# An output ring cut into three equal slots instead of four stores a tile

## The chip, the cores and the metric

The kernel runs on one core of one Trainium2 chip. The metric is the time of the core in microseconds (us), the median over several executions. One further execution is taken by the hardware profiler, which gives a page and a trace. Engines are named as the page names them: PE for matrix multiply, PEld for its weight loads, DVE for elementwise work, ACT, POOL, and SP, which here only issues transfers.

## What is computed

```python
# inputs (4096, 32, 64) f32, W (496, 64, 64) f32
i_idx, j_idx = np.triu_indices(32, k=1)          # the 496 pairs i < j
vi = inputs[:, i_idx, :]
vj = inputs[:, j_idx, :]
vdotw = jnp.einsum('bpd,pde->bpe', vi, W)
inter = vdotw * vj
return inter.reshape(B, -1)                      # (4096, 31744) f32
```

For each of 4096 batch rows and each pair (i, j) of 32 fields, field i (64 numbers) goes through the pair's 64x64 matrix and is multiplied elementwise with field j. The output holds 520 MB; the inputs hold 42 MB. So this kernel writes far more than it reads.

## The kernel before

The batch is cut into NT = 32 tiles of 128 rows, one row to a partition. A tile's output is 31744 columns wide: 496 units of D = 64 columns, one unit for each pair. Units are the measure of everything below.

For a field i, all its pairs (i, j) lie side by side, 31 - i units of them, and need the same left operand. Fields are taken two at a time: pair of fields p holds fields 2p and 2p+1, which lie in the upper and the lower 64 partitions of one transposed block of x. The matmul (L221) multiplies the transposed field with up to 512 columns of weights into one PSUM bank, for both fields into two neighbouring banks. The eight PSUM banks are handed out two at a time (`take_banks`), so PE can be four steps ahead of DVE.

DVE then multiplies both banks with the matching columns of x in one instruction and writes the product into the SBUF tile `ring`. The instruction of L231 writes two runs of columns at once, one for field 2p and one for field 2p+1, whose places in the output lie a whole row of pairs apart. L239 writes single runs, for the pieces that have no partner.

The order of work in a tile is p = 0 to 15, and in each p the column chunks from left to right. At p = 3 the second half of the tile's x is transposed on PE (L181) and copied out by ACT (L182), at p = 9 the first half of the next tile's x.

The `ring` holds 28160 columns (440 units) in each partition. The list STORES groups the field pairs into four stores a tile, of 118, 102, 123 and 153 units. Each store's place in the ring is taken when its first product is made: directly behind the store before, or at column 0 where it would not fit behind. A DVE instruction that writes to a place in the ring waits until the stores that last read that place have landed in HBM. After a group's last product the store is issued on SP (L245):

```python
        for s, group in enumerate(STORES):
            if at + store_w[s] > RING:
                at = 0
            osb = ring[:, at : at + store_w[s]]
            at += store_w[s]
```

A store is one transfer of 128 rows, one to a partition, each contiguous in SBUF and in HBM. Eight rows go to each of the 16 DMA engines.

Inputs come in beside this. The weights (8 MB) are loaded once, in five pieces, on SP at the start. Tiles of x go into three slots, some of them loaded from ACT's queue (L156) and 13 of them from POOL's queue (L117). The POOL loads spread their rows unevenly over the DMA engines, with small "nudge" transfers that set at which engine the next one begins. A load of x waits until DVE has done with the tile that was in its slot.

Of the kernel before, what the change touches and what calls it, by code (L numbers as in the profile page):

```python
# [9 lines left out]
F32 = mybir.dt.float32  # L10
ALU = mybir.AluOpType

P = 128
BANK = 512
BANKS = 8

STORES = [[0, 1], [2, 3], [4, 5, 6], [7, 8, 9, 10, 11, 12, 13, 14, 15]]

LOADS = [[0], [1], [2, 3], [4, 5, 6], [7, 8, 9, 10, 11, 12, 13, 14, 15]]


FIRST_HALF_AT, SECOND_HALF_AT = 9, 3
RING = 28160

DMA_ENGINES = 16
LIGHT = 4
# [7 lines left out]
def x_slots(NT):  # L34


    loads = [[(0, 0)]]
    for t in range(1, NT, 2):
        if t + 1 == NT:
            loads.append([(t, 1)])  # L40
        elif loads[-1][-1] == (t - 1, 2):
            loads.append([(t + 1, 0), (t, 1)])
        else:
            loads.append([(t, 1), (t + 1, 2)])
    return loads


@with_exitstack
def pair_bilinear_kernel(
    ctx: ExitStack,  # L50
    tc: tile.TileContext,
    x: bass.AP,
    w: bass.AP,
    out: bass.AP,
    F: int,
    D: int,
):

    nc = tc.nc
    NT = out.shape[1] * 2 // (F * (F - 1) * D)
    NPR = F // 2

    width = [(F - 1 - i) * D for i in range(F)]
    off = [sum(width[:i]) for i in range(F)]
    cols = sum(width)


    woff = [i % 2 * D + sum(width[i % 2 : i : 2]) for i in range(F)]
    store_w = [sum(width[2 * p] + width[2 * p + 1] for p in g) for g in STORES]

    const = ctx.enter_context(tc.tile_pool(name="const", bufs=1))
    psum = ctx.enter_context(tc.tile_pool(name="ps", bufs=1, space=bass.MemoryType.PSUM))

    ident = const.tile([P, P], F32, tag="ident", name="ident")
    make_identity(nc, ident)

    def runs(tl, a, b, n):  # L100

        ap = tl[:, a : a + n]
        return bass.AP(ap.tensor, ap.offset, [list(ap.ap[0]), [b - a, 2], list(ap.ap[1])])

    xbuf = const.tile([P, 3 * F * D], F32, tag="x", name="x")
    x_loads = x_slots(NT)
    pads = (DMA_ENGINES + 1) * PAD
    tile_sizes = [P * F * D + (pads if t in LIGHT_TILES else 0) for t in range(NT)]
    x_sizes = [sum(tile_sizes[t] for t, s in load) for load in x_loads]
    slot = {t: xbuf[:, ts(s, F * D)] for load in x_loads for t, s in load}  # L110

    nudges = [const.tile([DMA_ENGINES, 16], F32, tag=f"nudge{i}", name=f"nudge{i}") for i in range(2)]
    cursor = 0

    def from_pool(out, in_):

        tc.keep_in_program_order(nc.gpsimd.dma_start(out=out, in_=in_))  # L117

    def from_engine(e):

        nonlocal cursor
        k = (e - cursor) % DMA_ENGINES
        if k:
            nudge = nudges[e == LIGHT + 1]
            from_pool(
                nudge[:k].rearrange("p (h c) -> p h c", h=2)[:, :, :4],
                x[: k * 8].rearrange("(p h c) -> p h c", p=k, h=2),
            )
        cursor = e

    def load_beside(at, xt, lap):

        nonlocal cursor
        most = DMA_ENGINES - 1
        for e, k, rows, p in (
            (PAIRS_FROM[lap % len(PAIRS_FROM)], 2, REST, most * HEAD),
            (LIGHT + 1, most, HEAD, 0),
        ):
            from_engine(e)
            n = rows * F * D  # L140
            blocks = x[at : at + k * (n + PAD)].rearrange("(k c) -> k c", k=k)
            from_pool(xt[p : p + k * rows], blocks[:, :n])
            at += k * (n + PAD)
            cursor = (e + k) % DMA_ENGINES

    def load_x(load):

        at = sum(x_sizes[: x_loads.index(load)])
        parts = [[(t, s)] for t, s in load] if any(t in LIGHT_TILES for t, s in load) else [load]
        for part in parts:  # L150
            t, s = part[0]
            n = len(part) * F * D
            if t in LIGHT_TILES:
                load_beside(at, slot[t], LIGHT_TILES.index(t))
            else:
                nc.scalar.dma_start(  # L156
                    out=xbuf[:, s * F * D : s * F * D + n],
                    in_=x[at : at + P * n].rearrange("(p c) -> p c", p=P),
                )
            at += sum(tile_sizes[t] for t, s in part)  # L160

    pring = psum.tile([P, BANKS * BANK], F32, tag="pring", name="pring")
    bank = 0

    def take_banks(n):

        nonlocal bank
        if bank + n > BANKS:
            bank = 0
        got = pring[:, bank * BANK : (bank + n) * BANK]  # L170
        bank = (bank + n) % BANKS
        return got

    xT = const.tile([P, NPR * P], F32, tag="xT", name="xT")

    def transpose_x(xt, g):

        n = 2 * BANK // P
        pt = take_banks(2)
        for c in range(n):  # L180
            nc.tensor.transpose(pt[:, ts(c, P)], xt[:, ts(n * g + c, P)], ident)  # L181
        nc.scalar.copy(xT[:, ts(g, 2 * BANK)], pt)  # L182

    ring = const.tile([P, RING], F32, tag="ring", name="ring")
    at = 0

    load_x(x_loads[0])
    w_sb = const.tile([P, sum(width[0::2])], F32, tag="w", name="w")
    done = 0
    for g in LOADS:  # L190

        upto = woff[2 * g[-1]] + width[2 * g[-1]]
        nc.sync.dma_start(out=w_sb[:, done:upto], in_=w[:, done:upto])
        done = upto

    transpose_x(slot[0], 0)
    for t in range(NT):
        xt = slot[t]
        for load in x_loads:
            if min(load)[0] == t + 1:  # L200
                load_x(load)
        for s, group in enumerate(STORES):
            if at + store_w[s] > RING:
                at = 0
            osb = ring[:, at : at + store_w[s]]
            at += store_w[s]
            o0 = off[2 * group[0]]
            for p in group:
                if p == SECOND_HALF_AT:
                    transpose_x(xt, 1)  # L210
                if p == FIRST_HALF_AT and t + 1 < NT:
                    transpose_x(slot[t + 1], 0)
                first = (width[2 * p] - 1) % BANK + 1
                for c1 in range(first, width[2 * p] + 1, BANK):
                    n = first if c1 == first else BANK
                    c0 = c1 - n
                    odd = width[2 * p + 1] and c1 > D
                    pm = take_banks(2)
                    for h in range(1 + bool(odd)):
                        a = woff[2 * p + h] + c0 - h * D  # L220
                        nc.tensor.matmul(  # L221
                            pm[:, h * BANK : h * BANK + n],
                            xT[h * D : (h + 1) * D, ts(p, P)],
                            w_sb[h * D : (h + 1) * D, a : a + n],
                            start=True,
                            stop=True,
                        )
                    xj = xt[:, (2 * p + 1) * D + c0 : (2 * p + 1) * D + c1]
                    o = [off[2 * p + h] - o0 + c0 - h * D for h in range(2)]
                    if odd and (c0 or c1 < width[2 * p]):  # L230
                        nc.vector.tensor_tensor(  # L231
                            runs(osb, o[0], o[1], n),
                            runs(pm, 0, BANK, n),
                            bass.AP(xj.tensor, xj.offset, [xj.ap[0], [0, 2], xj.ap[1]]),
                            ALU.mult,
                        )
                    else:
                        for h in range(1 + bool(odd)):
                            nc.vector.tensor_tensor(  # L239
                                osb[:, o[h] + h * D : o[h] + n],  # L240
                                pm[:, h * (BANK + D) : h * BANK + n],
                                xj[:, h * D :],
                                ALU.mult,
                            )
            nc.sync.dma_start(  # L245
                out=out[:, t * cols + o0 : t * cols + o0 + store_w[s]], in_=osb
            )


# [46 lines left out]
```

## Time and profile before

| | |
|---|---|
| median of 6 runs | 1321.95 us (1320.86 to 1322.64) |
| the profiled execution's own time | 1322.64 us |
| its span on the page | 1320.5 us, so 2.1 us lie outside the span |
| granted PE clock, mean | 0.978 |
| PE, PEld busy | 1161.1 us (88%), 531.4 us (40%) |
| DVE busy | 1183.1 us (90%) in 1376 instructions |
| ACT, POOL busy | 66.1 us, 30.3 us |
| bytes | 41.95 MB read, 520.09 MB written, 426 GB/s over the span |
| stores | 128, from 3264 KB to 4896 KB each |

An engine's busy time is a share of the span, whatever it waited for. The DMA rows of the page show what the 16 DMA engines together did: their mean busy share in each fortieth of the span and the rate. A wait is put down to what ended it last.

### The profile page before, as it was taken

The numbers are of one execution on the slowest core, as the hardware profiler recorded it, in microseconds if no ns is written. First come the engines' busy times: TensorE is split into PE (matmuls) and PEld (weight loads), VectorE is DVE, ScalarE is ACT, GpSimd is POOL, SyncE is SP. The second block draws the span as 40 slices with busy tenths as digits, with TensorE's granted clock in tenths as the row PEclk, the third lists the DMA queues.
The fourth block names the chain that finished last, engine by engine and source line by source line (L and its number), as shares of the span: only waits on it lengthen the run. The fifth ranks groups of instructions, "written<-read, shape, count | busy, mean of one in ns | idle before, by whom it ended". The sixth has DMA issues, their size and how long they took to land.

```text
span 1320.5 us, 13176 instructions
## 1 busy us (share of the span) xinstructions
PE 1161.1 (88%) x5376; PEld 531.4 (40%) x5376; DVE 1183.1 (90%) x1376; ACT 66.1 (5%) x65; POOL 30.3 (2%) x58
## 2 busy tenths in 40 slices
PE   6998889889889898998898989898998989899893
PEld 3444344343444433443334434344443434344441
DVE  5998899989899998998899899898998989899994
ACT  1000000000000000000000000000000000000000
POOL 0000000000000000000000000000000000000000
PEclk9998999999999999999999999999999999999997
DMA  9999999999999999999999999999999999999998
GB/s 392 436 426 433 431 429 431 432 432 418 433 424 428 434 423 429 428 423 427 431 428 427 433 427 419 432 424 427 430 432 428 416 432 428 426 435 431 429 430 377
DMA packets 25404, 562.90 MB, mean 426 GB/s; under 512 B 4480, under 2 KB 4480, under 8 KB 4736
## 3 DMA queue, kind: packets, MB, share of 16 engines
q1 hardware_dynamic: 19152, 528.49, 93.5%
q10 hardware_dynamic: 2448, 19.92, 3.6%
q0 software_dynamic: 3744, 13.65, 2.6%
q8 instruction: 42, 0.69, 0.2%
q14 instruction: 18, 0.15, 0.0%
HBM read 41.95 MB, written 520.09 MB: 426 GB/s over the span
## 4 chain that ended last, share of the span: by engine, by line
DMA 48%; DVE 35%; issue 8%; PE 7%; DVEq 0%; ACT 0%
DMA out_dram<-ring 47%; DVE ring L231 30%; PE pring L221 7%; DVE ring L239 5%; DMA x<-in_x_dram 1%; PE pring L181 0%; DVEq L231 0%; ACT xT L182 0%; DVEq L292 0%; DVEq L239 0%
## 5 line engine op out<-in xcount | busy, mean ns | idle before, releaser
L221 PE MATMUL pring<-w,xT 64*128 64x512 f32 (+4 forms) x4864 | 1097.9, 559 | 130.8 <-DVE ring L231 111.9
L231 DVE TENSOR_TENSOR ring<-pring,x 128x1024 f32<-128x1024 f32 (+3 forms) x1056 | 1104.4, 1108 | 108.2 <-DMA out_dram<-ring 75.6
L221 PEld LDWEIGHTS pring<-w,xT 64*128 64x128 f32 x4864 | 475.9, 189 | 711.4 <-DVE ring L231 531.8
L182 ACT COPY xT<-pring 128x1024 f32<-128x1024 f32 x64 | 64.8, 1012 | 1209.6 <-PE pring L181 1209.6
L239 DVE TENSOR_TENSOR ring<-pring,x 128x64 f32<-128x64 f32 (+3 forms) x320 | 97.6, 355 | 11.4 <-DMA out_dram<-ring 11.2
L181 PEld LDWEIGHTS pring<-ident,x 128*128 128x128 f32 x512 | 55.5, 142 | 57.9 <-DVE ring L231 48.9
L181 PE MATMUL pring<-ident,x 128*128 128x128 f32 x512 | 70.8, 282 | 9.0 <-DMA x<-in_x_dram 9.0
L117 POOL DMA_DIRECT2D x<-in_x_dram x26 | 15.3, 587 | 1077.5 <-DVE ring L239 1077.2
L117 POOL DMA_DIRECT2D nudge<-in_x_dram x26 | 14.6, 561 | 0.3 <-issue 0.3
L182 ACT ACT_TABLE_LOAD x1 | 1.3, 1283 | 1.7 <-PEq L288 1.7
masks.py:199 POOL TENSOR_SCALAR_AFFINE_SELECT ident<-ident 128x128 f32<-128x128 f32 x1 | 0.3, 289 | 0.1
masks.py:197 POOL MEMSET ident<- 128x128 f32 x1 | 0.2, 205 | 0.3 <-POOLq L288 0.3
L288 POOL MEMSET const-float32-0.0<- 128x1 f32 x1 | 0.1, 99 | 0.2 <-issue 0.2
L288 POOL MEMSET const-bfloat16-1.0<- 128x1 bf16 x1 | 0.1, 102 | 0.0
L288 POOL MEMSET const-uint8-127<- 128x1 uint8 x1 | 0.1, 102 | 0.0
L288 POOL MEMSET const-float32-1.0<- 128x1 f32 x1 | 0.1, 99 | 0.0
## 6 DMA issues: line engine op xcount, KB each, us to landing
out_dram<-ring SPq DMA_DIRECT2D x32, 4896.0 KB, 18.1
out_dram<-ring SPq DMA_DIRECT2D x32, 3936.0 KB, 17.8
out_dram<-ring SPq DMA_DIRECT2D x32, 3776.0 KB, 19.8
out_dram<-ring SPq DMA_DIRECT2D x32, 3264.0 KB, 20.0
x<-in_x_dram ACTq DMA_DIRECT2D x15, 1024.0 KB, 18.6
x<-in_x_dram POOLq DMA_DIRECT2D x13, 960.0 KB, 26.4
x<-in_x_dram ACTq DMA_DIRECT2D x2, 2048.0 KB, 17.6
w<-in_w_dram SPq DMA_DIRECT2D x1, 2592.0 KB, 28.7
```

Of the source, the lines that this page charges most:

```text
L117: tc.keep_in_program_order(nc.gpsimd.dma_start(out=out, in_=in_))
L181: nc.tensor.transpose(pt[:, ts(c, P)], xt[:, ts(n * g + c, P)], ident)
L182: nc.scalar.copy(xT[:, ts(g, 2 * BANK)], pt)
L221: nc.tensor.matmul(pm[:, h * BANK : h * BANK + n], xT[h * D : (h + 1) * D, ts(p, P)], w_sb[h * D : (h + 1) * D, a : a + n], start=True, st ...
L231: nc.vector.tensor_tensor(runs(osb, o[0], o[1], n), runs(pm, 0, BANK, n), bass.AP(xj.tensor, xj.offset, [xj.ap[0], [0, 2], xj.ap[1]]), ALU ...
L239: nc.vector.tensor_tensor(osb[:, o[h] + h * D : o[h] + n], pm[:, h * (BANK + D) : h * BANK + n], xj[:, h * D :], ALU.mult,)
L288: nc = bacc.Bacc("TRN2", target_bir_lowering=False, num_devices=1)
```

## The change

The list STORES is gone, and with it the four places a tile. The ring keeps its 440 units and is now used as one endless strip: column c of the whole output (all tiles one after the other) lies at c modulo 440 units. Stores follow their own list of borders: four in the first round (118, 102, 110, 110 units), then in each round 147, 147 and 146, and a rest of 32 units at the end. A store may begin in one tile and end in the next. `made` counts for each store how much of it is still missing and issues it on SP when nothing is. `multiply` cuts a product in two where it would run over the end of the ring; where the second of its two runs comes to lie ahead of the first in the ring, it writes the runs by two instructions in place of one. Matmuls, transposes, loads and their order are as before.

```diff
-STORES = [[0, 1], [2, 3], [4, 5, 6], [7, 8, 9, 10, 11, 12, 13, 14, 15]]
+ROUND = [147, 147, 146]
+FIRST_ROUND = [118, 102, 110, 110]
-RING = 28160
+RING_UNITS = sum(ROUND)
...
+    ring_w = RING_UNITS * D
+    ends = [0]
+    while ends[-1] < NT * cols:
+        for units in ROUND if ends[-1] else FIRST_ROUND:
+            ends.append(min(ends[-1] + units * D, NT * cols))
+            if ends[-1] == NT * cols:
+                break
+    missing = [b - a for a, b in zip(ends, ends[1:])]
+    stored = 0
...
+    def multiply(tos, pm, xj, n):
+
+        at = [to % ring_w for to in tos]
+        cuts = {ring_w - a for a in at if a < ring_w < a + n}
+        for i, j in zip([0, *sorted(cuts)], [*sorted(cuts), n]):
+            a = [(to + i) % ring_w for to in tos]
+            if len(tos) == 2 and a[0] < a[1]:
+                xs = xj[:, i:j]
+                nc.vector.tensor_tensor(
+                    runs(ring, a[0], a[1], j - i),
+                    runs(pm, i, BANK + i, j - i),
+                    bass.AP(xs.tensor, xs.offset, [xs.ap[0], [0, 2], xs.ap[1]]),
+                    ALU.mult,
+                )
+                continue
+            for h, b in enumerate(a):
+                nc.vector.tensor_tensor(
+                    ring[:, b : b + j - i],
+                    pm[:, h * BANK + i : h * BANK + j],
+                    xj[:, i:j],
+                    ALU.mult,
+                )
+
+    def made(a, b):
+
+        nonlocal stored
+        for i in range(stored, len(missing)):
+            missing[i] -= max(0, min(b, ends[i + 1]) - max(a, ends[i]))
+        while stored < len(missing) and not missing[stored]:
+            a, b = ends[stored : stored + 2]
+            nc.sync.dma_start(
+                out=out[:, a:b], in_=ring[:, a % ring_w : a % ring_w + b - a]
+            )
+            stored += 1
...
-        for s, group in enumerate(STORES):
-            if at + store_w[s] > RING:
-                at = 0
...
+                o = [t * cols + off[2 * p + h] + c0 - h * D for h in range(2)]
+                if odd and (c0 or c1 < width[2 * p]):
+                    multiply(o, pm, xj, n)
+                else:
                     for h in range(1 + bool(odd)):
+                        multiply([o[h] + h * D], pm[:, h * (BANK + D) :], xj[:, h * D :], n - h * D)
+                for h in range(1 + bool(odd)):
+                    a = o[h] + (0 if c0 else h * D)
+                    made(a, o[h] + n)
-            nc.sync.dma_start(
-                out=out[:, t * cols + o0 : t * cols + o0 + store_w[s]], in_=osb
-            )
```

More of the change, by code (lines that the diff above doesn't have):

```diff
@@ L91, in pair_bilinear_kernel @@
     woff = [i % 2 * D + sum(width[i % 2 : i : 2]) for i in range(F)]
-    store_w = [sum(width[2 * p] + width[2 * p + 1] for p in g) for g in STORES]
+    ring_w = RING_UNITS * D
[7 more added lines that the diff above has]
+    stored = 0
     const = ctx.enter_context(tc.tile_pool(name="const", bufs=1))
@@ L182, in transpose_x @@
         nc.scalar.copy(xT[:, ts(g, 2 * BANK)], pt)
-    ring = const.tile([P, RING], F32, tag="ring", name="ring")
-    at = 0
+    ring = const.tile([P, ring_w], F32, tag="ring", name="ring")
+    def multiply(tos, pm, xj, n):
[29 more added lines that the diff above has]
+            stored += 1
     load_x(x_loads[0])
@@ L201, in pair_bilinear_kernel @@
                 load_x(load)
-        for s, group in enumerate(STORES):
-            if at + store_w[s] > RING:
[L204 to L218, printed above, removed]
-                    for h in range(1 + bool(odd)):
[L220 to L226, printed above, removed]
-                        )
[L228 to L244, printed above, removed]
-            nc.sync.dma_start(
-                out=out[:, t * cols + o0 : t * cols + o0 + store_w[s]], in_=osb
-            )
@@ new lines, in pair_bilinear_kernel @@
+        for p in range(NPR):
+            if p == SECOND_HALF_AT:
+                transpose_x(xt, 1)
+            if p == FIRST_HALF_AT and t + 1 < NT:
+                transpose_x(slot[t + 1], 0)
+            first = (width[2 * p] - 1) % BANK + 1
+            for c1 in range(first, width[2 * p] + 1, BANK):
+                n = first if c1 == first else BANK
+                c0 = c1 - n
+                odd = width[2 * p + 1] and c1 > D
+                pm = take_banks(2)
+                for h in range(1 + bool(odd)):
+                    a = woff[2 * p + h] + c0 - h * D
+                    nc.tensor.matmul(
+                        pm[:, h * BANK : h * BANK + n],
+                        xT[h * D : (h + 1) * D, ts(p, P)],
+                        w_sb[h * D : (h + 1) * D, a : a + n],
+                        start=True,
+                        stop=True,
+                    )
+                xj = xt[:, (2 * p + 1) * D + c0 : (2 * p + 1) * D + c1]
+                o = [t * cols + off[2 * p + h] + c0 - h * D for h in range(2)]
+                if odd and (c0 or c1 < width[2 * p]):
+                    multiply(o, pm, xj, n)
+                else:
+                    for h in range(1 + bool(odd)):
+                        multiply([o[h] + h * D], pm[:, h * (BANK + D) :], xj[:, h * D :], n - h * D)
+                for h in range(1 + bool(odd)):
+                    a = o[h] + (0 if c0 else h * D)
+                    made(a, o[h] + n)
```

## The prediction

> **What bounds it now.** I read the page first: the 40 slices, the queues, then the chain.
>
> ```profile
> DVE  5998899989899998998899899898998989899994
> ...
> DMA  9999999999999999999999999999999999999998
> GB/s 392 436 426 433 431 429 431 432 432 418 433 424 428 434 423 429 428 423 427 431 428 427 433 427 419 432 424 427 430 432 428 416 432 428 426 435 431 429 430 377
> ...
> q1 hardware_dynamic: 19152, 528.49, 93.5%
> q10 hardware_dynamic: 2448, 19.92, 3.6%
> q0 software_dynamic: 3744, 13.65, 2.6%
> ...
> HBM read 41.95 MB, written 520.09 MB: 426 GB/s over the span
> ...
> DMA 48%; DVE 35%; issue 8%; PE 7%; DVEq 0%; ACT 0%
> ```
>
> The DMA row never leaves 9 until the last slice, and the three queues' packets add up to 99.7% of 16 engines' span. The chain (last line) gives DVE 35% and could mislead: it follows waits, and DVE's work lies between two waits for a store. So I asked what DVE waits for (us in total, times, longest), and took the DMA share by stretches (the columns after the times are PE, PEld, DVE, ACT, POOL, granted clock, DMA share, GB/s):
>
> ```profile
> DVE ring L231 <- DMA out_dram<-ring: 75.6, 42, 5.0
> DVE ring L239 <- DMA out_dram<-ring: 11.2, 7, 2.3
> ```
>
> ```profile
> 540.00:640.00 100.00, 89.28 (x419) 41.26 (x417) 91.61 (x105) 5.06 (x5) 2.26 (x4) 0.98 1.00 426
> ...
> 1240.00:1290.00 50.00, 45.27 (x208) 20.41 (x206) 46.10 (x53) 2.03 (x2) 0.00 (x0) 0.97 1.00 429
> 1290.00:1320.50 30.50, 9.25 (x48) 4.02 (x44) 12.40 (x19) 0.00 (x0) 0.00 (x0) 0.72 0.86 372
> ```
>
> DVE has 86.8 us to spare in waits for ring space, and the DMA share is 1.00 up to the tail. The kernel is bound by its transfers, whose bytes the change leaves alone. What can still move is what the transfers cost beyond their bytes, and the little time in which a DMA engine stands idle. I count against the profiled execution (1322.64 us, span 1320.5; 0.69 above the median 1321.95) and carry the difference to the median. A difference under 0.2% (2.6 us) is about what a measurement of this kernel cannot tell from none.
>
> **Fewer stores.** The order of instructions shows 110 stores in place of 128, of 37632 or 37376 bytes a row. In the trace's packet records a row of 26112 bytes takes 968 ns, one of 39168 takes 1448: 36.8 ns per 1000 bytes and 8 ns for the row itself. Rows start 3 ns before the one before has ended, so a row costs 5 ns beyond its bytes, and the 9 ns completion packet behind each store's eight rows 6. Eighteen stores fewer: 18 x (8 x 5 + 6) = 828 ns on every engine, all on the path: **-0.8 us**. The Trainium skill (DMA: Bandwidth & Descriptors, Anatomy of one DMA) has a fixed cost of about 2.0 us a transfer, fitted on another issue path; charged to 18 stores that would be 36 us, but the rows of one store follow the last store's at once here, so it is hidden. The same page's Rules for kernel authors ask for 1 MiB a transfer at least, which 3264 KB already exceed, and speak against any gain.
>
> **More DVE instructions.** 1483 in place of 1376, because runs are cut at the ring's end or written singly behind it. From start to start 1024 columns take 1131 ns and 64 take 131: 64 ns an instruction beyond its columns. 107 x 64 = 6.8 us, hidden by the 86.8 us of waits; uncovered it would cost those 6.8 us, once DVE waited for nothing. PE has the same 2944 matmuls and holds a pair of banks 64 ns longer at 107 places. Instruction fetch (42 packets of 16 KB, 940 ns each) grows by one packet at most: 0 to 0.9 us on one engine; I take 0, since 107 instructions are under 1% of 13176.
>
> **Other waits for ring space.** This is the part with a sign to find. After DVE's last wait ahead of a store, so much of its work is left until the store can be issued; meanwhile the engines live on the stores already queued. I went through the order of DVE's instructions with the times above (4% added, as DVE's busy time is about that much above the sum of them). Before, the worst is the 153-unit store in every third tile: it needs the landing of the store two back and then 3.6 us of DVE work, beside 9.3 us of queued rows (8 x 1166 ns), a cover of 5.7 us; the median is 8.0. After, a border can fall inside long rows, where DVE must write far into the next slot to finish this one: up to 4.6 us of work, but beside a whole slot of 11.0 us. The worst cover is 6.5, the median 9.4. The larger stores make up for the crossing.
>
> From the cover go 0.5 us from a last row's end to landing, some 0.9 us from issue to the first row, and the spread of the 16 engines: at a landing the first is 3 to 5 us ahead of the last. So before, 5.7 - 1.4 = 4.3 us does not quite feed the foremost engines, and the packet records show it: nine short spells with idle engines between 40 and 1290 us (near 296, 377, 418, 459, 539, 578, 782, 905 and 1147), each at the issue of a 153-unit store, 1.8 us in all as a mean of 16 engines. Never more than 10 of the 16 were idle. After, 6.5 - 1.4 = 5.1 us feeds nearly all. But the end is set by the last engine, which is not the one that was starved. At the last landing (1319.5 us) the next three engines came 0.7 to 0.9 us before it, so speeding up one engine gains no more than 0.7. Bounds 0 and -1.8; I take **-0.7 us**, from those landings.
>
> **Start, end, loads.** DMA engines are never idle from 2.5 us on, so an earlier third store (110 units for 123) gains nothing. At the end the last store shrinks from 153 units to 32, but the last one was issued at 1302.7 while the one before landed at 1307.9: the engines had no gap to close, and have none after, with a slot of 11 us still queued. SP carries only these stores after the weights, in order, so nothing is queued behind a later one but the next store. Loads of x take turns with store rows: eight rows of 309 ns each behind one of 1448 (beside a 153-unit store) make 14.1 us, after 13.6 (1392), and at most 13.6 for 11.4 beside the 118-unit store: +2.2 us later. The load issued at 577.7 landed at 598.2 and was read by the transposes at 609.7: 11.5 us of cover. Zero.
>
> **Sum**: -0.8 - 0.7 = -1.5 us: profiled execution 1321.1, span 1319.0, median **1320.4 us**.
>
> **Rivals.** *Stalls go too (faster).* Between 40 and 1290 us store rows took 8.9 us more than their usual time, as a mean of 16 engines; 2.8 us of it falls within 25 us behind one of the nine idle spells. If engines that restart together hinder each other, spells and stalls go: -0.8 - 1.8 - 2.8 = -5.4, 1316.5. Against it: tiles without a spell have such stalls too (0.55 us near 1040), always beside loads of x.
>
> *Longer rows stall more (slower).* The excess per row was 2.8 ns at 26112 bytes, 9.5 at 30208, 5.0 at 31488, 18.6 at 39168. If size makes it, 37632 lies at 15.9, and 848 rows an engine lose 13.5 us for 8.9: +4.6 - 1.5 = +3.1, 1325.0. It decides from 12.3 ns a row ((8.9 + 1.5) / 848) and shows as slower from 15.4. Against it: the order is not that of sizes, and the 153- and 118-unit stores are the ones that run beside loads of x.
>
> *The ring does not do what it says*, its slots being released as a whole: excluded, since the order shows one store's landing in each of DVE's ring waits.
>
> **Numbers.** The sum's own case lies between -0.8 - 1.8 = -2.6 (1319.4) and -0.8 + 0.9 = +0.1 (1322.1); it has 0.50, and all of it is under 0.2%. Stalls go, wholly or by half: 0.34. Longer rows: 0.16. Those are the chances of same, faster and slower. The range runs to both rivals, 1316.5 to 1325.0.
>
> **What would show it.** Right: 110 stores; DVE's waits for the ring lower by some 7 us; the DMA share 1.00 throughout; no spell of idle engines of the size of that at 578. Excess per store row near 10 ns, whatever the size, speaks for the sum; 15 or more for the slower rival; 5 for the faster one. Wrong: a DMA share under 1.00 in a stretch of the middle, or PE waiting for x.

## The result and the profile after

The changed kernel's median is 1319.52 us (21 runs, 1317.64 to 1324.44) against 1322.45 us (42 runs) for the kernel before, run beside it. The ratio is 0.9982 with a 95% interval of 0.9976 to 0.9988: 2.4 us less (1.6 to 3.2); the two medians themselves lie 2.9 us apart. The prediction said 1.5 us less, and held differences under 2.6 us to be about what a measurement of this kernel cannot tell from none. With this many runs the interval is 0.8 us to either side, so this one can be told. The profiled execution took 1318.22 us with a span of 1316.4, so this one execution gained 4.4 us, more than the medians. Some 0.35 us of the difference to the kernel before, here and in all the experiments, arises outside the span: 2.1 to 2.2 us lie outside it in each execution of the kernel before, 1.7 to 1.9 us in each one of the changed kernel and of the variants. No run shows why.

The page of the changed kernel: slices, queues and chain, as shown of the kernel before.

```profile
DVE  5999899998998989989899898989989899999993
...
DMA  9999999999999999999999999999999999999998
GB/s 394 427 433 434 431 431 431 427 436 426 430 432 426 426 432 429 431 430 433 430 430 430 432 428 430 432 425 430 429 432 427 430 425 431 425 431 437 432 429 370
...
q1 hardware_dynamic: 16560, 528.49, 93.5%
q10 hardware_dynamic: 2448, 19.92, 3.6%
q0 software_dynamic: 3744, 13.65, 2.6%
...
HBM read 41.95 MB, written 520.09 MB: 427 GB/s over the span
...
DMA 55%; DVE 33%; issue 6%; PE 5%; DVEq 0%; ACT 0%
```

The DMA row looks the same as before, and it must: the engines were busy before and are busy now. The rate row tells more. Its low slices in the middle, 416 to 419 before, are gone; the lowest is 425. The q1 row has 2592 packets less for the same bytes (18 stores of 128 rows and 16 completions each).

DVE's waits for ring space (us in total, times, longest), then three stretches (the columns as before: PE, PEld, DVE, ACT, POOL, granted clock, DMA share, GB/s):

```profile
DVE ring L203 <- DMA out_dram<-ring: 49.2, 32, 5.1
...
DVE ring L211 <- DMA out_dram<-ring: 19.5, 16, 3.6
```

```profile
540.00:640.00 100.00, 90.19 (x412) 44.32 (x412) 91.44 (x117) 5.07 (x5) 2.26 (x4) 0.96 1.00 430
1240.00:1290.00 50.00, 46.15 (x214) 20.46 (x212) 48.69 (x61) 2.02 (x2) 0.00 (x0) 1.00 1.00 431
1290.00:1316.40 26.40, 2.81 (x18) 1.37 (x14) 4.94 (x12) 0.00 (x0) 0.00 (x0) 0.59 0.83 359
```

The waits fell from 86.8 to 68.7 us, and at a DMA share of 1.00 the stretch from 540 to 640 us moved 430 GB/s in place of 426. A share of 1.00 therefore does not say that the bytes flow at one rate: a row that takes longer than usual counts as busy too.

So I made a ledger from the packet records, as a mean of the 16 engines: what rows and completions cost beyond their bytes, by how much store rows exceeded the usual time of their size (close to 8 ns plus 36.8 ns per 1000 bytes; from 40 us to 30 us before the end; below, stalls), what all rows of x took (less the 3 ns by which each begins before the last packet's end), in how much of the same stretch engines stood idle, and how far the last engine ended behind the mean. Two profiles of each kernel:

| us | rows and completions | stalls | rows of x | idle spells | mean end | last end |
|---|---|---|---|---|---|---|
| before | 6.8 | 8.9 | 79.0 | 1.8 | 1316.6 | 1319.0 |
| before, again | 6.8 | 9.3 | 79.4 | 2.6 | 1318.7 | 1321.4 |
| changed | 6.0 | 7.1 | 79.3 | 0.1 | 1312.8 | 1314.9 |
| changed, again | 6.0 | 7.4 | 79.1 | 0.2 | 1313.4 | 1316.2 |

Three terms moved: -0.8, about -1.9 and -1.7 to -2.4. If the first four columns are taken off the mean end, 1220.1 to 1220.7 us are left in all four profiles, so these columns account for what the mean engine gained to within 0.6 us.

They account for single executions, though. The two of the kernel before took 0.2 and 2.1 us more than the median of the runs beside them, the two of the changed kernel 1.3 and 0.2 us less. So the pairs lie 4.4 and 5.4 us apart, about twice the 2.4 us of all runs. How these 2.4 us divide among the three terms is not shown.

### The profile page after: what moved, and what is told of

It is laid out like the page before. It is cut to its first block, busy times and chain, and to the rows that moved or that the text cites. A ratio compares the mean times of both kernels' runs of the same rounds, so it can differ in the third digit from the quotient of the medians.

```text
span 1316.4 us, 13188 instructions
## 1 busy us (share of the span) xinstructions
PE 1176.9 (89%) x5376; PEld 553.4 (42%) x5376; DVE 1190.3 (90%) x1483; ACT 66.1 (5%) x65; POOL 30.3 (2%) x58
## 4 chain that ended last, share of the span: by engine, by line
DMA 55%; DVE 33%; issue 6%; PE 5%; DVEq 0%; ACT 0%
DMA out_dram<-ring 54%; DVE ring L203 27%; DVE ring L211 5%; PE pring L258 4%; DMA x<-in_x_dram 1%; PE pring L190 0%; DVEq L203 0%; ACT xT L191 0%; DVEq L319 0%; DVEq L211 0%
## 5 line engine op out<-in xcount | busy, mean ns | idle before, releaser
L258 PE MATMUL pring<-w,xT 64*128 64x512 f32 (+4 forms) x4864 | 1113.7, 561 | 99.7 <-DVE ring L203 80.9
L203 DVE TENSOR_TENSOR ring<-pring,x 128x1024 f32<-128x1024 f32 (+4 forms) x1012 | 1043.9, 1092 | 84.1 <-DMA out_dram<-ring 49.2
L258 PEld LDWEIGHTS pring<-w,xT 64*128 64x128 f32 x4864 | 497.8, 190 | 673.9 <-DVE ring L203 477.7
L211 DVE TENSOR_TENSOR ring<-pring,x 128x64 f32<-128x64 f32 (+7 forms) x471 | 169.3, 412 | 20.5 <-DMA out_dram<-ring 19.5
L190 PE MATMUL pring<-ident,x 128*128 128x128 f32 x512 | 71.4, 282 | 16.2 <-DMA x<-in_x_dram 8.6
```

Source lines behind the costliest of these rows:

```text
L203: nc.vector.tensor_tensor(runs(ring, a[0], a[1], j - i), runs(pm, i, BANK + i, j - i), bass.AP(xs.tensor, xs.offset, [xs.ap[0], [0, 2], xs ...
L211: nc.vector.tensor_tensor(ring[:, b : b + j - i], pm[:, h * BANK + i : h * BANK + j], xj[:, i:j], ALU.mult,)
L258: nc.tensor.matmul(pm[:, h * BANK : h * BANK + n], xT[h * D : (h + 1) * D, ts(p, P)], w_sb[h * D : (h + 1) * D, a : a + n], start=True, st ...
```

## The experiments

All edits but the last start from the changed kernel. A ratio is to the kernel before, run beside it.

**The two kernels once more.** For the changed kernel:

> The changed kernel itself once more: a second profile for the size of what differs from run to run. The stalls (rows above their usual time) fell from 8.9 to 7.1 us in the first pair of profiles. If that belongs to the change, it is near 7 again, and the time 0.18% under the kernel before; if it is scatter, it may be 9.

Measured: ratio 0.9981 (0.9969 to 0.9992), stalls 7.4 us. For the kernel before:

> The kernel before once more, for a second profile: the idle spells come back at the 153-unit stores, 1.5 to 2 us as a mean of the engines, and the stalls are near 8.9 us, if both belong to the kernel and not to the one execution.

Measured: one execution of 1324.95 us, with 2.6 us of idle spells between 377 and 1110 us and 9.3 us of stalls; one spell, near 1024 us, makes 1.2 of the 2.6. In two executions of each kernel, then, spells and stalls went with the kernel.

**Two slots in place of three.**

```diff
-ROUND = [147, 147, 146]
+ROUND = [220, 220]
```

> The same ring of 440 units in two slots of 220 in place of three: 75 stores in place of 110. Queue theory (the engines must be fed while DVE fills a slot): after the landing of the store two back only 16.5 us of rows are queued, and DVE needs up to a whole slot of work; the cover is -1.8 us at the median store, less 1.4 us from landing and issue, so each of some 70 stores leaves the engines idle for about 3 us: about +220 us, some 1540 us, with the DMA share near 0.85. Rival (fewer, larger stores are what helps): 35 stores less at 46 ns: -1.6 us against the changed kernel, 1318.

Measured: 1529.13 us, ratio 1.1551 (1.1530 to 1.1572). The stretch from 540 to 640 us:

```profile
540.00:640.00 100.00, 83.01 (x360) 41.24 (x358) 80.32 (x102) 4.05 (x4) 0.00 (x0) 0.90 0.87 371
```

The DMA share is 0.87, and the idle spells are 176 us. The cover (the queued rows less DVE's work, as the prediction counts it) gave 1540 us. Fewer stores are worth nothing once the queue runs dry.

**Four slots of 110 units.**

```diff
-ROUND = [147, 147, 146]
+ROUND = [110, 110, 110, 110]
```

> The same ring in four slots of 110 units: 145 stores in place of 110, rows of 28160 bytes. Packet theory (46 ns a store on every engine, nothing else left to gain from cover): +35 x 46 = +1.6 us against the changed kernel, 1321.1; no idle spells, since the cover is 14.7 us at the median. Row-size theory (longer rows stall more): rows of 28160 lie between 2.8 and 9.5 ns of excess a row, so excess falls from 7.1 us to about 4 in the sum of store rows, 1319.5 + 1.6 - 3 = 1318.

Measured: 1318.62 us, ratio 0.9968 (0.9956 to 0.9979). Idle spells 0.00, stalls 5.5 us: 35 stores more cost 1.6 us in the ledger, and stalls and rows of x gave back 2.2. The packet theory alone (1321.1) is wrong; what it left out is the stalls. The row-size theory's 1318 is what came, but two experiments below speak against its reason. The size of this kernel's stalls depends on what is called usual: against the commonest time of its 28160-byte rows, 1044 ns, they are 4.7 us.

**Three slots of 124 units, a ring of 372.**

```diff
-ROUND = [147, 147, 146]
-FIRST_ROUND = [118, 102, 110, 110]
+ROUND = [124, 124, 124]
+FIRST_ROUND = [118, 102, 76, 76]
```

> The changed kernel with a ring of 372 units in three slots of 124: what the ring before used in the mean, and 129 stores, as many as before, but all of one size and crossing the borders of tiles. Queue and packet theory: +0.9 us for 19 stores more than the changed kernel, and cover down to 6.0 us at the worst (6.5 in the changed kernel, 5.7 before), so some of the idle spells come back, 0.3 to 1 us as a mean of the engines: between 1320.4 and 1321.5. If the equal slots or the crossing alone were the gain, it stays at 1319.5; if the space in the ring alone, it goes to the time before, 1322.4.

Measured: 1317.45 us, ratio 0.9960 (0.9947 to 0.9972). All three expectations missed: with as many stores as before and less ring it is faster than the changed kernel. Idle spells 0.1, stalls 5.4. It was run again beside the last three experiments below:

> Three slots of 124 units once more, for its interval beside the others on one chip: 1317.5, 0.4% under the kernel before, if the first result holds; near 1319.5 if it was luck of the last engine.

Measured: 1318.50 us, ratio 0.9965 (0.9953 to 0.9977), stalls 5.5, idle 0.1. It holds; this version beats both kernels.

**All runs written singly.**

```diff
-            if len(tos) == 2 and a[0] < a[1]:
+            if False:
```

> Every pair of runs is written by two DVE instructions: 2497 of them in place of 1483, 1014 x 64 ns = 65 us more DVE work, stores and ring as in the changed kernel. If DVE's work hides under its waits for ring space (68.7 us there), nearly all of the waits go and the time rises by no more than what single stores lose locally, 0 to 8 us: 1320 to 1328. If DVE's work were on the path, the 107 instructions of the change cost 6.8 us that something else repaid, and these cost 65: 1385.

Measured: 1326.32 us, ratio 1.0025 (1.0016 to 1.0033). The page's row of busy times and the only wait of DVE for the ring:

```profile
PE 1238.4 (94%) x5376; PEld 751.9 (57%) x5376; DVE 1250.6 (95%) x2495; ACT 66.1 (5%) x65; POOL 30.2 (2%) x58
```

```profile
DVE ring L211 <- DMA out_dram<-ring: 27.5, 28, 2.5
```

DVE has 60 us more to do than in the changed kernel, its waits for the ring shrink by 41, and the time grows by some 6 us (the ratio by 0.0043), inside the 0 to 8 expected. Most of the 60 us, then, lay beside the transfers, and so did most of the 6.8 us that the 107 instructions of the change cost DVE: a tenth of these 6 us would be 0.6. The profile shows the 6 us as some 2.8 us more in rows of x, 0.4 more of idle spells, and a last engine that ends 4.9 us behind the mean, where it was 2.1 and 2.8.

**Two stores to a slot.**

```diff
-            nc.sync.dma_start(
-                out=out[:, a:b], in_=ring[:, a % ring_w : a % ring_w + b - a]
-            )
+            half = a + (b - a) // (2 * D) * D
+            for a, b in ((a, half), (half, b)):
+                nc.sync.dma_start(
+                    out=out[:, a:b], in_=ring[:, a % ring_w : a % ring_w + b - a]
+                )
```

> The changed kernel with each slot stored by two transfers of half its columns, issued together when the slot is full: 220 stores in place of 110, rows of about 18.8 KB. Packet theory: 110 x (8 x 5 + 6) = 5.1 us more on every engine: 1324.6. Row-size theory: rows of half the size have hardly any excess, so some 5 us go while 5.1 come: 1319 to 1320. If the rows' own cost were hidden, no change: 1319.5.

Measured: 1321.44 us, ratio 0.9991 (0.9982 to 1.0000), 1.7 us above the changed kernel. Both theories are half right. Rows and completions go from 6.0 to 11.1 us in the ledger; that is the count of packets at the prices worked out before, and the price of a row holds at half the size (695 ns at 18688 bytes). The stalls go from 7.1 to 3.9. The mean engine of the profile ends 2.9 to 3.5 us later than in the two profiles of the changed kernel. That is more than these two terms make, and the rest lies in the last 30 us, which the ledger's idle column leaves out: there the engines stood idle for 2.7 us on average before their ends, 0.4 and 0.5 in the changed kernel. The edit also frees ring space by halves, which the expectation did not reckon with: the worst cover is 12 us.

**The tile's own stores in the endless ring.**

```diff
-    ends = [0]
-    while ends[-1] < NT * cols:
...
+    in_tile = [0, 118 * D, 220 * D, 343 * D]
+    ends = sorted(
+        {t * cols + c for t in range(NT) for c in in_tile}
+        | {*range(0, NT * cols, ring_w)}
+        | {NT * cols}
+    )
```

> The ring is used to its end as in the changed kernel, but stores end where they did before (118, 102, 123, 153 units in each tile), and a store that runs over the ring's end is cut in two there: 164 or so stores. The endless ring alone, without the three slots. Sum by packets and cover: 54 stores more than the changed kernel at 46 ns, +2.5 us: 1322.0, with hardly any idle spells. If the spells are worth more than the 0.7 us that the prediction gave them, the 1.7 us of packets against the kernel before is outweighed and it comes out at 1321 or below; if they are worth nothing, 1322.4 + 1.7 = 1324.

Measured: 1325.03 us, ratio 1.0017 (1.0004 to 1.0030): 3 us above the sum, nearest to the 1324 expected if the spells were worth nothing, and not faster than the kernel before. That does not settle what the spells are worth, since they came back here. One spell near 1145 us makes 1.6 of the 2.2 us of idle time, although the worst cover is 10.8 us: from 1129 to 1157 us the last engine landed 7 to 10 us after the median one, and a store frees its place only when its last engine has landed. At the end the last engine is 5.6 us behind the mean. The use of the ring to its end is not by itself the gain.

**Three slots of 134 units.**

```diff
-ROUND = [147, 147, 146]
-FIRST_ROUND = [118, 102, 110, 110]
+ROUND = [134, 134, 134]
+FIRST_ROUND = [118, 102, 91, 91]
```

> Three slots of 134 units (ring of 402), between the changed kernel's 147 and the 124 of the run with a ring of 372: 120 stores, rows of 34304 bytes, worst cover 5.6 us. Ledger theory (time = bytes + 46 ns a store + stalls that grow with the row's length beside loads of x + idle spells): +0.5 us of stores, stalls near 6.2 us in place of 7.1 to 7.4, idle under 0.5: 1318.7, between the two. If 124 is fast because it divides a tile's 496 units, and not for its length, 134 is no faster than 147: 1319.6.

Measured: 1328.01 us, ratio 1.0037 (1.0023 to 1.0051). Missed by 9 us: a size between two good ones is worse than both. Two stretches:

```profile
540.00:640.00 100.00, 88.74 (x414) 41.80 (x411) 91.19 (x113) 5.06 (x5) 2.25 (x4) 0.97 1.00 422
1040.00:1140.00 100.00, 88.62 (x403) 38.79 (x400) 89.62 (x109) 4.05 (x4) 1.72 (x3) 0.98 1.00 421
```

The share is 1.00 again, at 422 GB/s in place of 430. Idle spells are 3.2 us, stalls 8.0, and the rows of x take 83.7 us in place of 79.3. With 0.5 us for ten stores more, this makes 8.9 us beside the changed kernel, and the mean engine did end 8.9 us later (1321.7 us). Row length alone does not set the stalls, then: these rows are shorter than the changed kernel's, and their stalls are no smaller.

**Three slots of 104 units.**

```diff
-ROUND = [147, 147, 146]
-FIRST_ROUND = [118, 102, 110, 110]
+ROUND = [104, 104, 104]
+FIRST_ROUND = [118, 102, 92]
```

> Three slots of 104 units (ring of 312): 153 stores, rows of 26624 bytes. Row length alone would go on to lower the stalls, to about 4.5 us, against +2.0 us of stores: 1318.5. Queue theory: the cover falls to 3.3 us at the worst and 6.2 at the median, with 31 stores under 5.0, where the kernel before had ten of 5.7 and 1.8 to 2.6 us of idle spells: 5 to 10 us of spells as a mean of the engines, 1322 to 1327.

Measured: 1327.53 us, ratio 1.0039 (1.0025 to 1.0053). The time is as the queue theory had it, 9 us above what row length alone would give, but the idle spells are only 1.3 us. Its queues (packets, MB, share of 16 engines):

```profile
q1 hardware_dynamic: 22752, 528.49, 93.2%
q10 hardware_dynamic: 2448, 19.92, 3.6%
q0 software_dynamic: 3744, 13.65, 3.0%
```

The same q0 packets, the loads of x from POOL's queue, take 3.0% in place of 2.6% of the span: a row of 8192 bytes took 370 ns in the mean, 313 in the changed kernel. All rows of x take 85.4 us, 6 more.

The packet records show where these rows are slow. A packet begins within a few ns of the end of the one before it on its engine, which puts the packets in line engine by engine. With 104-unit slots 793 of the 1664 rows of this queue came directly behind another row of the same queue, and took 427 ns in the mean; behind a store row they took 314. In the changed kernel 238 did, at 320 ns against 309; with 134-unit slots 447, at 384, and with all runs written singly 466, at 380. Such rows make almost all of the 6 us here. A row of x meets its like when no store row stands between, so this too looks like a price of a short queue of stores, one that the idle spells do not show.

**The kernel before with five stores a tile.**

```diff
-STORES = [[0, 1], [2, 3], [4, 5, 6], [7, 8, 9, 10, 11, 12, 13, 14, 15]]
+STORES = [[0, 1], [2, 3], [4, 5, 6], [7, 8], [9, 10, 11, 12, 13, 14, 15]]
```

> The kernel before with one edit: the 153-unit store of each tile's end is two stores, of 62 and 91 units; nothing crosses a tile, and the ring is not used to its end. 160 stores, +32 x 46 ns = +1.5 us; the worst cover is 9.3 us, so no idle spells (1.8 to 2.6 us before); rows of 39168 bytes, which carry 4.6 of the 8.9 us of stalls, become rows of 15872 and 23296: about 3 us less. Ledger theory: 1322.5 + 1.5 - 3 - 0.7 = 1320.3 or below. If the use of the ring to its end were what counts, it loses the 1.5 us: 1324.

Measured: 1322.29 us, ratio 0.9994 (0.9982 to 1.0005), no difference, where the ledger theory had 1320.3 and its rival 1324. Its ledger is what was expected: idle 0.0, stalls 6.3, rows and completions +1.5, the mean engine's end at 1313.8, within 1 us of the changed kernel. But in this profile the last engine ends 4.6 us behind the mean (2.4 and 2.7 before), and that eats most of the gain.

All of it in one table, ordered by the worst cover, which is worked out as in the prediction (us; where a kernel was profiled twice, both values):

| kernel | stores | worst cover | idle spells | rows of x | stalls | last behind mean | ratio |
|---|---|---|---|---|---|---|---|
| two stores a slot | 220 | 12.1 | 0.0 | 78.7 | 3.9 | 1.9 | 0.9991 |
| four slots of 110 | 145 | 12.1 | 0.0 | 78.7 | 5.5 | 2.2 | 0.9968 |
| tile stores, endless ring | 164 | 10.8 | 2.2 | 78.9 | 7.6 | 5.6 | 1.0017 |
| five stores a tile | 160 | 9.3 | 0.0 | 79.1 | 6.3 | 4.6 | 0.9994 |
| all runs singly | 110 | 6.7 | 0.5 | 82.0 | 7.3 | 4.9 | 1.0025 |
| changed | 110 | 6.5 | 0.1, 0.2 | 79.3, 79.1 | 7.1, 7.4 | 2.1, 2.8 | 0.9982 |
| three slots of 124 | 129 | 6.0 | 0.1, 0.1 | 79.4, 79.5 | 5.4, 5.5 | 2.1, 2.2 | 0.9960 |
| before | 128 | 5.7 | 1.8, 2.6 | 79.0, 79.4 | 8.9, 9.3 | 2.4, 2.7 | 1 |
| three slots of 134 | 120 | 5.6 | 3.2 | 83.7 | 8.0 | 4.8 | 1.0037 |
| three slots of 104 | 153 | 3.3 | 1.3 | 85.4 | 7.0 | 2.0 | 1.0039 |
| two slots of 220 | 75 | -4.6 | 176 | 101.5 | 22.2 | 1.8 | 1.1551 |

## Why the prediction was right, and where it was short

The sum's 1.5 us lie just under the measured 1.6 to 3.2. In the profiles its two terms are there, beside a third that it had put at nothing.

**Fewer stores, -0.8 us.** Right, as far as packets show it: 18 stores at the price of their rows and completions, and that price held for 110 stores more. The fixed cost of about 2.0 us a transfer that the Trainium skill gives for another issue path (DMA: Bandwidth & Descriptors, Anatomy of one DMA), charged to each store in turn, would have made 110 more stores cost 220 us. The run with two stores a slot rose by 1.7. Where stores queue behind each other, the measurement decides against charging it so.

**DVE, nothing.** Right. Its busy time rose from 1183.1 to 1190.3 us, 7.2 for the 6.8 worked out, and nearly ten times the dose cost some 6 us in all. Its waits for the ring fell by 18.1 us, not by 7: the longer work and the shorter span (4.1) make 11.3 of it, waits for PE that grew from 21.8 to 25.2 us another 3.4, and the rest was not followed.

**Idle spells.** The mechanism was right (and the prediction's "never idle from 2.5 us on" too strong beside its own nine spells): they were at the 153-unit stores, and went from 1.8 and 2.6 us to 0.1 and 0.2. In the table the step lies between a cover of 5.7 and of 6.0 us, where the prediction led one to look, as long as the last engine stays near the others. Below it the spells are not the whole price: with 3.3 us of cover they were 1.3 us, and the rows of x took 6 us more. What the spells are worth in time was taken as 0.7 us of at most 1.8. The runs do not separate that share: the mean engine gained all of the 1.7 to 2.4, and how much of it reaches the last one changes from run to run.

**Stalls, taken as zero.** This is the term that was short. They fell by 1.8 and 1.9 us in the two pairs of profiles. The faster rival foresaw 2.8 together with all of the idle time, which in sum (-5.4) was too much for the medians and not far from the profiled executions (-4.4 and -5.4). So in size the truth lay between the sum and this rival. The rival's reason, that engines which restart together hinder each other, is not what moves them: with 124-unit slots the spells are 0.1 us as in the changed kernel, and the stalls fall from 7.1 to 5.4 all the same.

**Longer rows stall more.** The price of this rival fails: it needed 15.9 ns a row of 37632 bytes, and 7.9 and 8.3 came out (9.5 and 9.9 for the rows of 37376), less than the 18.6 of the 39168-byte rows before. Size alone is out too, by the 134-unit slots, whose 34304-byte rows stalled by 8.8 ns. What the prediction held against the rival was the better lead. I split store rows by whether a row of x was moving on any engine at the same time. Outside such stretches they stalled by 4.1 and 4.4 ns in the mean before and by 4.3 and 4.2 after (but by 12 and 14 for the 39168-byte rows, few of which lay outside). Within, it was 18.0 and 18.7 before, 14.9 and 16.2 in the changed kernel, 9.4 with slots of 124, 7.9 with four slots, and 2.7 with half slots. Before, the stores of 153 and 118 units were the ones that met the loads. So some 70% of the stalls lie beside loads of x, and the new borders changed which rows meet them. What sets their size there is open. Length does not order it: 34304-byte rows (134 units) had 17.8 ns and 26624-byte rows (104 units) 14.7, more than the 28160-byte rows of four slots. All this was only read from profiles; no run took the loads away.

**What stays open.** Which engine ends last and why. It ended 1.8 to 2.8 us behind the mean in seven of the kernels and 4.6 to 5.6 in the other four, one of which, five stores a tile, lost most of its gain by it. The wide scatter of the changed kernel's times, 1317.6 to 1324.4, against 1317.3 to 1319.4 for the 124-unit slots, may be the same thing; the profiles, of one execution each, cannot show it. Why 134 units are so much worse than 124, which divide a tile's 496 into four and so meet each tile's loads at the same place, is not settled either. The phase against the loads fits, but was not tested alone, and dividing 496 is not needed: slots of 110 do not, and gave 0.9968, with a cover of 12.1 us. The worst cover of 134 units, 5.6 us, is below that of 124, 6.0, but hardly below the 5.7 of the kernel before.

## What to carry to other kernels

When the transfers are busy all the time, count what remains: the fixed cost of each store, rows that take longer than usual, and engines that stand idle, and look at the rate beside the busy share, which cannot tell a flowing row from a stalled one. Size a ring of stores by its cover, the queued rows at a landing less the work until the next store, and hold it above the spread of the DMA engines plus the way from landing to first row (here about 6 us, and more where one engine falls far behind). Beyond that, a store less gains 46 ns, and this can be outweighed: slots of 124 and 110 units, with 19 and 35 stores more, beat those of 147, with smaller stalls. Try neighbouring sizes on the chip before settling on one: 147, 134, 124 and 110 units gave 0.9982, 1.0037, 0.9960 and 0.9968.

## What the runs showed of the hardware

- A store row costs 5 ns beyond its bytes and a store's completion 6 ns on each engine, from rows of 18.7 KB to 39 KB (695 ns at 18688 bytes, 1448 at 39168).
- A row of 8192 bytes on POOL's queue took 313 ns in the mean in the changed kernel, 370 with slots of 104 units and 518 with two slots, where the queue ran dry. The slow ones are those that come directly behind another row of their own queue on an engine: 427 ns with slots of 104 units, against 314 behind a store row.
- The 16 engines, given the same bytes of each store, drift apart. Between the first and the last to land one store lay up to 5.3 and 7.1 us in the kernel before, and up to 12.5 with tile stores in the endless ring. The drift was least where the engines ran out of stores: at the median store 1.9 us with two slots, 3.7 in the kernel before, 5.1 in the changed kernel and 7.1 with five stores a tile. The slowest engine sets both the landing of each store and the end.
